# Delta rule in a four-layer kernel: chunks in two halves by turns, small sums in PSUM, query sums on TensorE, waves in half steps

## The chip, the cores and the metric

The kernel runs on one core of a Trainium2 chip. It is written out instruction by instruction: TensorE (PE) multiplies matrices into PSUM, VectorE (DVE) and ScalarE (ACT) work on SBUF and PSUM, GpSimd (POOL) works on SBUF alone, and SyncE (SP) issues most DMAs. The metric is the device time of one execution in microseconds.

## The reference

Four transformer-like layers work on 4096 tokens of 128 features. The change lies in the fourth, which adds two branches to its input: a gated delta rule with 16 heads of 8 dimensions, and a feed-forward network with a sine in it. Cut to what matters:

```python
def step(S, inp):                       # 1024 steps, 4 x 16 independent heads, S is 8 x 8
    q_t, k_t, v_t, b_t = inp
    v_new = (v_t - einsum('bhd,bhdm->bhm', k_t, S)) * b_t[..., None]
    S = S + einsum('bhd,bhm->bhdm', k_t, v_new)
    o_t = einsum('bhd,bhdm->bhm', q_t, S)
    return (S, o_t)
...
imag = w_imag * sin(theta + hidden * 0.1)          # hidden = x @ W1 + b1, 512 wide
q = hidden + (cos(theta) * w_real + sin(theta) * w_imag) * imag * 0.1
out = relu(q) @ W2 + b2
```

Queries and keys are divided by their norms over the 8 dimensions. The outputs of a head are normalised afterwards and multiplied by a last matrix.

## The kernel before

**The delta rule.** The 1024 steps are cut into 32 chunks of 32 steps (`CH` and `N` in `_delta_rule`, L1749). All chunks go through their steps side by side. A state tile has 128 partitions (head and batch, times two halves of the 8 value dimensions) and 1024 columns: 32 chunks of 4 values by 8 key dimensions. It lies in two PSUM banks, chunks 0 to 15 in one and 16 to 31 in the other.

One step of the rule is `differ` (L1853) with `update` (L1868). DVE multiplies the state in PSUM by the keys (`pro`, L1859), and sums the products over the 8 key dimensions (`dd`, L1862). With values it subtracts these (L1865), and it multiplies the difference by the keys (`u`, L1870). PE writes the state anew: `add` (L1847) multiplies a copy of the old state by the identity, and `u` by the negative identity, into the same PSUM tile. Each `add` is two matmuls, one for each bank, and the profile shows two records of each matmul. ACT makes the copy of the state (`copy`, L1874).

Three stretches follow one another on the same tiles:

- The chunk products: 32 iterations (L1898), each with two steps. One (`sm`) turns unit matrices into each chunk's product, the other (`sn`) gives what the chunk makes of a zero state. They alternate, so that PE works on one while DVE works on the other. From the ninth iteration on, `query_norms` (L1889) lets ACT square a block of queries, and DVE reduces the block of the iteration before (L1896, eight times).
- The scan over chunks (L1921): 31 small steps on DVE alone, each two products, a sum and an addition (L1924 to L1932), in SBUF. Ahead of it the rows of `mm` are exchanged between partition halves by DMA, and the inverse norms of the queries are formed (L1917, with the helper at L1783).
- The steps from the scan's states (L1944): 32 steps of the rule for all chunks at once, `pro` in two instructions. In each, GpSimd multiplies the state's copy by the queries (`dprod`, L1965), and DVE sums the products two iterations later (L1941). A one-element GpSimd copy from `u` into `pace` (L1963) stands ahead of the product in GpSimd's queue.

**The waves.** `_waves` (L1970) is the sine network: 32 items of 128 x 512. An item passes through five stages: `enter` (matmul into `qh`, three ACT operations that give argument and number of turns), `fold` (DVE takes off the turns and clamps, L2013 and L2014; ACT forms the sine), `rest` (DVE L2019, ACT Relu), `leave` (matmul into `qo`) and `close` (DVE adds four items' result to `x`, L2030). A wave step runs `close`, `leave`, `rest`, `fold`, `enter`, each on a different item.

**The order.** Layer 3 is recorded under `manual_schedule` (L2105): PE, DVE, ACT and POOL run their instructions in the order in which Python issues them, and the tile layer adds only semaphores. A wait therefore holds everything behind it on its engine. Two accesses of different engines to one PSUM bank are put one after the other. `_delta_rule` is a generator, and the loop at its call decides after which of its yields a wave step follows:

```python
for n, _ in enumerate(_delta_rule(k, s, wl)):
    if n % 2 if n < 32 or n >= 63 else n % 6 == 2:
        next(waves, None)
```

Yields 0 to 31 are those of the chunk products, 32 to 62 those of the scan, and the later ones those of the last 32 steps. The wave steps fall 16 in the first stretch, 6 beside the scan and 14 in the last.

Of the kernel before, what the change touches and what calls it, by code (L numbers as in the profile page):

```python
# [20 lines left out]
P = 128  # L21
# [196 lines left out]
def _bc(ap, axis, n):  # L218

    ap = ap.unsqueeze(axis)  # L220
    shape = list(ap.shape)
    shape[axis] = n
    return ap.to_broadcast(shape)
# [1525 lines left out]
def _delta_rule(k, s, wl):  # L1749
# [7 lines left out]
    CH = 32  # L1757
# [89 lines left out]
    def add(st, w, u, first, last):  # L1847

        c = u.shape[1]
        for n in (slice(0, 16), slice(16, c)):  # L1850
            nc.tensor.matmul(st[:, n], w, u[:, n], start=first, stop=last)  # L1851

    def differ(st, now, i, c, values, parts=1):  # L1853


        pro = room("pro")
        for n in range(parts):
            own = slice(n * c // parts, (n + 1) * c // parts)
            nc.vector.tensor_tensor(pro[:, own], st[:, own], _bc(kp[:, i, own], 2, 4), ALU.mult)  # L1859
        add(st, k.ident, now()[:, :c], True, False)  # L1860
        d = w.tile([P, CH, 4], F32, name="dd")
        nc.vector.tensor_reduce(d[:, :c], pro[:, :c], AX.X, ALU.add)  # L1862
        yield
        if values:
            nc.vector.tensor_tensor(d[:, :c], d[:, :c], vp[:, i, :c], ALU.subtract)  # L1865
        yield update(st, d, i, c)

    def update(st, d, i, c, first=False):  # L1868
        u = room("u")
        nc.vector.tensor_tensor(u[:, :c], _bc(d[:, :c], 3, 8), _bc(kp[:, i, :c], 2, 4), ALU.mult)  # L1870
        add(st, k.neg_ident, u[:, :c], first, True)
        return u

    def copy(name, st, c):  # L1874
        now = room(name)
        nc.scalar.copy(flat(now[:, :c]), flat(st[:, :c]))  # L1876
        return now
# [6 lines left out]
    ends = CH - 1  # L1884
    add(sm, k.ident, _bc(k.unit.rearrange("p (v d) -> p v d", d=8), 1, ends), True, True)
    mm, nn = copy("hist", sm, ends), None
    squares = ip.tile([P, 4, 8, P], F32, name="dvo")

    def query_norms(c):  # L1889
        if 0 <= c < 8:  # L1890
            own = slice(c * P, (c + 1) * P)
            nc.scalar.activation(squares[:, c % 4], qraw[:, :, own], AF.Square)
        if 1 <= c < 9:
            own = slice((c - 1) * P, c * P)
            sq = squares[:, (c - 1) % 4]
            nc.vector.tensor_reduce(rq[:, own], sq.rearrange("p d t -> p t d"), AX.X, ALU.add)  # L1896

    for i in range(N):  # L1898
        for _ in differ(sm, lambda: mm, i, ends, False):
            pass  # L1900
        mm = copy("hist", sm, ends)
        if i:
            for _ in differ(sn, lambda: nn, i, ends, True):
                pass
        else:
            d = w.tile([P, CH, 4], F32, name="dd")
            nc.vector.tensor_scalar(d[:, :ends], vp[:, 0, :ends], -1.0, None, ALU.mult)
            update(sn, d, 0, ends, True)
        nn = copy("dprod", sn, ends)
        query_norms(i - 8)  # L1910
        yield

    both = [room("u") for _ in range(2)]
    for m in range(2):
        for other in range(2):
            nc.sync.dma_start(both[m][HALF[other], :ends], mm[HALF[m], :ends])
    inverse(rq)  # L1917
    nc.vector.tensor_scalar(rq, rq, 8.0**-0.5, None, ALU.mult)
    start = ip.tile([P, L], F32, name="from_unit").rearrange("p (c v d) -> p c v d", v=4, d=8)
    nc.vector.memset(start[:, 0], 0.0)  # L1920
    for c in range(CH - 1):  # L1921
        pro = w.tile([P, 4, 2, 4, 8], F32, name="scan")
        for m in range(2):
            nc.vector.tensor_tensor(  # L1924
                pro[:, :, m],
                _bc(both[m][:, c], 1, 4),
                _bc(start[:, c, :, 4 * m : 4 * m + 4], 3, 8),
                ALU.mult,
            )
        r = w.tile([P, 4, 8], F32, name="scan_r")  # L1930
        nc.vector.tensor_reduce(r, pro.rearrange("p v m j d -> p v d (m j)"), AX.X, ALU.add)  # L1931
        nc.vector.tensor_tensor(start[:, c + 1], r, nn[:, c], ALU.add)  # L1932
        yield
    oc = ip.tile([P, N, CH, 4], F32, name="dvo")
    st = states("sm")
    add(st, k.ident, start, True, True)
    q_at = qraw.rearrange("p d (c i) -> p c d i", i=N)
    hist, prod = None, None

    def output(i):  # L1940
        nc.vector.tensor_reduce(oc[:, i], prod, AX.X, ALU.add)  # L1941


    for i in range(N + 1):  # L1944
        if i < N:
            hist = None

            def now():
                nonlocal hist
                hist = copy("hist", st, CH) if i else start  # L1950
                return hist

            step = differ(st, now, i, CH, True, 2)
            next(step)
            yield
            u = next(step)
        else:
            u, hist = None, copy("hist", st, CH)
        if i >= 2:
            output(i - 2)  # L1960
        if i:
            if u is not None:
                nc.gpsimd.tensor_copy(s.pace, u[:, 0, 0, 0:1])  # L1963
            prod = room("dprod")
            nc.gpsimd.tensor_tensor(prod, hist, _bc(q_at[:, :, :, i - 1], 2, 4), ALU.mult)  # L1965
    output(N - 1)
# [3 lines left out]
def _waves(k, a, s):  # L1970
# [26 lines left out]
    nc.vector.scalar_tensor_tensor(argb, k.vec("l3_b1"), 0.1, theta, ALU.mult, ALU.add)  # L1997
    b1 = k.vec("l3_b1")
# [3 lines left out]
    def enter(z):  # L2002
        z.one = slice(z.f, z.f + 1)
        z.hp = s.q_ps.tile([P, W], F32, name="qh")
        nc.tensor.matmul(z.hp, w1[:, z.f * P : (z.f + 1) * P], k.xn[:, z.c], start=True, stop=True)
        z.arg = xp.tile([P, W], F32, name="qarg")
        nc.scalar.activation(z.arg, z.hp, AF.Identity, bias=argb[:, z.one], scale=0.1)
        z.turns = xp.tile([P, W], F32, name="qtmp", bufs=2)
        nc.scalar.activation(z.turns, z.arg, AF.Identity, bias=rnd[:, 0:1], scale=1.0 / TWO_PI)
        nc.scalar.activation(z.turns, z.turns, AF.Identity, bias=rnd[:, 1:2])  # L2010

    def fold(z):
        nc.vector.scalar_tensor_tensor(z.arg, z.turns, -TWO_PI, z.arg, ALU.mult, ALU.add)  # L2013
        nc.vector.tensor_scalar(z.arg, z.arg, PI_F32, -PI_F32, ALU.min, ALU.max)  # L2014
        nc.scalar.activation(z.arg, z.arg, AF.Sin)
# [18 lines left out]
    stages = (enter, fold, rest, leave, close)  # L2034
    for n in range(len(items) + 4):
        for m in (4, 3, 2, 1, 0):
            if 0 <= n - m < len(items):
                stages[m](items[n - m])
        yield
# [47 lines left out]
def _layer3(k, a, out):  # L2087
    nc, tc = k.nc, k.tc
    with ExitStack() as stack:
# [17 lines left out]
        s.pace = s.ip.tile([P, 1], F32, name="pace")  # L2107
        with ExitStack() as banks:
# [6 lines left out]
            s.st_ps, s.q_ps, s.q_out = bank("st_ps", 1), bank("q_ps", 3), bank("qo_ps", 1)  # L2115
            waves = _waves(k, a, s)
            for n, _ in enumerate(_delta_rule(k, s, wl)):
                if n % 2 if n < 32 or n >= 63 else n % 6 == 2:
                    next(waves, None)
# [80 lines left out]
```

## Time and profile before

| what | us |
|---|---|
| median of three runs | 4837.96 (4836.27 to 4839.41) |
| profiled execution | 4844.06 |
| its span | 4842.3 |
| from the first `pro` to the last `u` of the chunk products | 281.8 |
| from there to the scan | 16.7 |
| scan | 52.0 |
| from the first `pro` to the last `u` of the last steps | 241.3 |
| from there to the output's scaling | 8.9 |

Over the whole span PE is busy 81%, DVE 65%, ACT 53% and POOL 14%, but most of this is in the layers before. In the listings, a timeline's line gives the start (us from the span's start), the duration, the engine, the line of the kernel, the operation, and output and inputs by tile; the brackets at the end give the idle time of the engine before it and what released it. Consecutive instructions of one kind may be merged (x2). Successive DVE instructions overlap a little, so that the time from one start to the next is what counts. In the groups, busy time and mean duration (ns) stand after the bar.

### The profile page before, as it was taken

The page shows a single profiled execution, that of the slowest core. Times are in us where ns is not written, and L with a number is a line of the kernel's source. Part 1 is how long each engine was busy: PE and PEld are TensorE (multiplying, and loading weights), DVE is VectorE, ACT ScalarE, POOL GpSimd, SP SyncE. Part 2 cuts the span into 40 slices and gives each one's busy share as a digit, 9 for nine tenths or more (in the row PEclk, how much of TensorE's full clock was granted, in tenths as well). Part 3 has the DMA queues.
Part 4 walks back from the last instruction along what each step waited for, and adds up shares of the span by engine and source line. Part 5 has one row for each costly group of instructions (what it writes and reads, how often), then busy time and mean ns, then how long its engine had stood idle before and what let it go on. Part 6 is the DMA issues. An engine that isn't in the chain of part 4 may idle for free. (4 is left out here: it accounts for less than half of the span.)

```text
span 4842.3 us, 54404 instructions
## 1 busy us (share of the span) xinstructions
PE 3915.2 (81%) x20918; PEld 1780.8 (37%) x20918; DVE 3134.4 (65%) x4431; ACT 2564.8 (53%) x3611; POOL 660.3 (14%) x647
## 2 busy tenths in 40 slices
PE   4679999998968888888877888888776975889565
PEld 3223333364422222222224555555432453333121
DVE  4868989622345565656558888887572323799876
ACT  1257877831269999999965555545311110344331
POOL 1310000003100000000003223232004023000132
PEclk6689999999967777777779999999888986999788
DMA  2412120021221010100011111111001122400001
GB/s 106 117 40 58 25 63 20 11 77 43 12 81 57 18 57 9 53 18 18 9 58 32 35 36 42 35 37 31 20 3 45 44 73 60 121 0 9 0 0 52
DMA packets 112742, 196.99 MB, mean 41 GB/s; under 512 B 23266, under 2 KB 53474, under 8 KB 110498
## 3 DMA queue, kind: packets, MB, share of 16 engines
q1 hardware_dynamic: 103860, 168.86, 12.4%
q0 software_dynamic: 8192, 16.79, 1.8%
q10 hardware_dynamic: 432, 7.86, 0.4%
q8 instruction: 165, 2.70, 0.2%
q14 instruction: 93, 0.76, 0.1%
HBM read 97.56 MB, written 70.01 MB: 35 GB/s over the span
## 5 line engine op out<-in xcount | busy, mean ns | idle before, releaser
L738 DVE TENSOR_TENSOR p<-p,e 128x1024 f32<-128x1024 f32 x512 | 586.6, 1222 | 322.3 <-ACT e L736 322.3
L721 PE MATMUL big<-q,k 32*128 32x512 f32 x2048 | 561.2, 633 | 180.4 <-ACT p L732 75.4
L531 DVE TENSOR_REDUCE m<-mx 128x2 f32<-128x1024 f32 x512 | 620.9, 1224 | 101.7 <-PE mx L523 94.3
L416 PE MATMUL av<-p,v 128*32 128x256 f32 (+1 forms) x5632 | 667.0, 530 | 0.2
L614 ACT ACTIVATE p<-s 128x512 f32<-128x512 f32 x1024 | 551.6, 598 | 187.0 <-PE s L605 173.0
L721 PEld LDWEIGHTS big<-q,k 32*128 32x128 f32 x2048 | 210.3, 229 | 708.1 <-ACT e L736 353.6
L605 PE MATMUL s<-q,k 64*128 64x512 f32 x1024 | 278.6, 494 | 46.6 <-DMA q<-mrows 31.7
L736 ACT ACTIVATE e<-big,neg_mu 128x1024 f32<-128x1024 f32 x256 | 262.2, 1126 | 11.8 <-PE big L721 11.6
L523 PE MATMUL mx<-k,q 64*128 64x512 f32 x1024 | 239.4, 437 | 32.3 <-DVE m L531 17.9
L732 ACT ACTIVATE p<-big,neg_mu 128x1024 f32<-128x1024 f32 x256 | 261.3, 1198 | 3.5 <-PE big L721 3.3
L736 ACT ACTIVATE e<-big 128x1024 f32<-128x1024 f32 x256 | 242.8, 1042 | 28.0 <-PE big L721 26.9
L732 ACT ACTIVATE p<-big 128x1024 f32<-128x1024 f32 x256 | 239.6, 1076 | 8.4 <-PE big L721 8.2
L1163 POOL TENSOR_TENSOR lqk<-lt 128x512 f32<-128x512 f32 x128 | 162.6, 1270 | 517.9 <-DVE lt L1154 460.8
L1136 PE MATMUL lps<-f_wqkv,lh 128*128 128x512 f32 x384 | 215.3, 649 | 11.1 <-DVE lo L1291 6.8
L1851 PE MATMUL sm<-hist,in_const_sb 128*128 128x512 f32 x252 | 140.6, 686 | 92.7 <-ACT hist L1876 79.1
L416 PEld LDWEIGHTS av<-p,v 128*32 128x32 f32 x5632 | 121.1, 112 | 254.6 <-issue 203.2
L605 PEld LDWEIGHTS s<-q,k 64*128 64x128 f32 x1024 | 108.0, 184 | 284.6 <-issue 162.5
L1017 POOL DMA_INDIRECT cl_row<-res,back x128 | 121.5, 949 | 621.9 <-DMA in_l_su_sb<-in_l_su 476.0
L1254 ACT ACTIVATE lsm<-lsm 128x512 f32<-128x512 f32 x128 | 80.9, 632 | 221.8 <-DVE lsm L1253 220.3
L1876 ACT COPY hist<-sm 128x992 f32<-128x992 f32 (+1 forms) x65 | 65.0, 1000 | 216.4 <-DVE pro L1859 133.6
L936 POOL DMA_INDIRECT buf<-xtok,to x128 | 123.7, 966 | 359.2 <-DVE gkern L1609 169.7
L1129 POOL MEMSET lva<- 128x32 f32 x16 | 2.4, 151 | 1147.9 <-PE av L416 1147.9
(403 smaller groups left out, 6960.5 us busy)
## 6 DMA issues: line engine op xcount, KB each, us to landing
hl<-phi SPq DMA_DIRECT2D x64, 256.0 KB
hl<-plo SPq DMA_DIRECT2D x64, 256.0 KB
lvs<-lva SPq DMA_DIRECT2D x16, 520.0 KB
q<-hl SPq DMA_DIRECT2D x32, 256.0 KB
k<-hl SPq DMA_DIRECT2D x32, 256.0 KB
q<-hl SPq DMA_DIRECT2D x16, 512.0 KB
k<-hl SPq DMA_DIRECT2D x16, 512.0 KB
buf<-zeros ACTq DMA_DIRECT2D x3, 2560.0 KB
```

What stands on the lines that cost most here:

```text
L416: k.nc.tensor.matmul(av[32 * j : 32 * j + 32, cols], v[:, kc, 9 * (4 * g + j) : 9 * (4 * g + j) + 32], pts[j][:, cols], start=kc == 0, sto ...
L523: nc.tensor.matmul(ps[:, i, :], q[rows, gg, qt * P : (qt + 1) * P], key[rows, gg, half * W : (half + 1) * W], start=True, stop=True, tile_ ...
L531: nc.vector.tensor_reduce(m[:, qt, gg, :, half], ps, AX.X, ALU.max)
L605: nc.tensor.matmul(ps, key[rows, half, kc * P : (kc + 1) * P], q[rows, half, qh * W : (qh + 1) * W], start=True, stop=True, tile_position= ...
L614: nc.scalar.activation(p, ps, AF.Exp, scale=8.0**-0.5)
L721: nc.tensor.matmul(ps[:, jj, :], key[rows, kc * P : (kc + 1) * P], q[rows, qh * W : (qh + 1) * W], start=True, stop=True, tile_position=(3 ...
L732: nc.scalar.activation(p, ps, f, bias=bias, scale=scale)
L736: nc.scalar.activation(e, ps, f, bias=bias, scale=scale)
L738: nc.vector.tensor_tensor(p, p, e, ALU.mult)
L1136: nc.tensor.matmul(ps, z.h[:, t * P : (t + 1) * P], wqkv[:, own], start=True, stop=True)
L1163: nc.gpsimd.tensor_tensor(z.qk[t][:, own], r[0], r[1], ALU.add)
L1851: nc.tensor.matmul(st[:, n], w, u[:, n], start=first, stop=last)
```

## The change

- In the last 32 steps, each step is made once for chunks 0 to 15 and once for 16 to 31 (`own`), each half with its own bank: `pro`, copy, identity `add`, `dd`, subtraction, `u`, negative `add`. The output sum and a yield stand behind the first half. The loop has 33 rounds with two yields each. `pace` is gone.
- The small sums `dd` of all stretches, and those of the scan, are written to PSUM, to four slices by turns (`turn`) of one tile in one bank. The scan's states are written straight to the PSUM tile `sm`, from which the last steps go on; the `add` that carried them there is gone.
- The queries' squares are summed by eight matmuls with the identity into such a slice, and ACT copies the result to `rq`. The square root follows in the 19th iteration of the chunk products. Behind them, one DVE operation clamps and scales, and a reciprocal follows.
- In the waves, argument and turns are kept in units of a turn, so that `fold` becomes a plain subtraction on GpSimd. The clamp and the sine are a new stage `sine`. A wave is two half steps with a yield each: `close`, `leave`, `rest`, `sine`, and then `enter`, `fold`. A half step follows every odd yield, and every yield of the scan: 16 half steps in the chunk products, 31 beside the scan, and the last 25 (of 72) in the last steps. `qh` has two PSUM buffers instead of three, `dd` takes the bank.

```diff
-    def add(st, w, u, first, last):
-        c = u.shape[1]
-        for n in (slice(0, 16), slice(16, c)):
-            nc.tensor.matmul(st[:, n], w, u[:, n], start=first, stop=last)
-    def differ(st, now, i, c, values, parts=1):
+    turns = itertools.cycle(range(4))
+    dd = s.d_ps.tile([P, 4, CH, 4], F32, name="dd")
+    turn = lambda: dd[:, next(turns)]
+    def add(st, w, u, own, first, last):
+        for n in (slice(0, 16), slice(16, CH)):
+            n = slice(max(n.start, own.start), min(n.stop, own.stop))
+            if n.start < n.stop:
+                nc.tensor.matmul(st[:, n], w, u[:, n], start=first, stop=last)
+    def differ(st, now, i, own, values):
         pro = room("pro")
-        for n in range(parts):
-            own = slice(n * c // parts, (n + 1) * c // parts)
-            nc.vector.tensor_tensor(pro[:, own], st[:, own], _bc(kp[:, i, own], 2, 4), ALU.mult)
-        add(st, k.ident, now()[:, :c], True, False)
-        d = w.tile([P, CH, 4], F32, name="dd")
-        nc.vector.tensor_reduce(d[:, :c], pro[:, :c], AX.X, ALU.add)
-        yield
+        nc.vector.tensor_tensor(pro[:, own], st[:, own], _bc(kp[:, i, own], 2, 4), ALU.mult)
+        add(st, k.ident, now(), own, True, False)
+        d = turn()
+        nc.vector.tensor_reduce(d[:, own], pro[:, own], AX.X, ALU.add)
         if values:
-            nc.vector.tensor_tensor(d[:, :c], d[:, :c], vp[:, i, :c], ALU.subtract)
-        yield update(st, d, i, c)
+            nc.vector.tensor_tensor(d[:, own], d[:, own], vp[:, i, own], ALU.subtract)
+        update(st, d, i, own)
...
         if 1 <= c < 9:
             own = slice((c - 1) * P, c * P)
-            sq = squares[:, (c - 1) % 4]
-            nc.vector.tensor_reduce(rq[:, own], sq.rearrange("p d t -> p t d"), AX.X, ALU.add)
+            sums = turn().rearrange("p c v -> p (c v)")
+            for d in range(8):
+                nc.tensor.matmul(sums, k.ident, squares[:, (c - 1) % 4, d], start=d == 0, stop=d == 7)
+            nc.scalar.copy(rq[:, own], sums)
...
         query_norms(i - 8)
+        if i == 18:
+            nc.scalar.activation(rq, rq, AF.Sqrt)
         yield
...
-    inverse(rq)
-    nc.vector.tensor_scalar(rq, rq, 8.0**-0.5, None, ALU.mult)
-    start = ip.tile([P, L], F32, name="from_unit").rearrange("p (c v d) -> p c v d", v=4, d=8)
-    nc.vector.memset(start[:, 0], 0.0)
+    nc.vector.tensor_scalar(rq, rq, 1e-6, 8.0**0.5, ALU.max, ALU.mult)
+    nc.vector.reciprocal(rq, rq)
+    st = states("sm")
+    nc.vector.memset(st[:, 0], 0.0)
     for c in range(CH - 1):
...
-                _bc(start[:, c, :, 4 * m : 4 * m + 4], 3, 8),
+                _bc(st[:, c, :, 4 * m : 4 * m + 4], 3, 8),
                 ALU.mult,
             )
-        r = w.tile([P, 4, 8], F32, name="scan_r")
+        r = turn().rearrange("p c v -> p (c v)")[:, :32].rearrange("p (v d) -> p v d", d=8)
         nc.vector.tensor_reduce(r, pro.rearrange("p v m j d -> p v d (m j)"), AX.X, ALU.add)
-        nc.vector.tensor_tensor(start[:, c + 1], r, nn[:, c], ALU.add)
+        nc.vector.tensor_tensor(st[:, c + 1], r, nn[:, c], ALU.add)
         yield
-    st = states("sm")
-    add(st, k.ident, start, True, True)
+    both_halves = slice(0, CH // 2), slice(CH // 2, CH)
...
     for i in range(N + 1):
-        if i < N:
-            hist = None
-            def now():
-                nonlocal hist
-                hist = copy("hist", st, CH) if i else start
-                return hist
-            step = differ(st, now, i, CH, True, 2)
-            next(step)
-            yield
-            u = next(step)
-        else:
-            u, hist = None, copy("hist", st, CH)
-        if i >= 2:
-            output(i - 2)
+        hist = room("hist")
+        for half, own in enumerate(both_halves):
+            if i < N:
+                differ(st, lambda: copy(hist, st, own), i, own, True)
+            else:
+                copy(hist, st, own)
+            if half == 0 and i >= 2:
+                output(i - 2)
+            if half == 0:
+                yield
         if i:
-            if u is not None:
-                nc.gpsimd.tensor_copy(s.pace, u[:, 0, 0, 0:1])
             prod = room("dprod")
             nc.gpsimd.tensor_tensor(prod, hist, _bc(q_at[:, :, :, i - 1], 2, 4), ALU.mult)
+        yield
...
     def fold(z):
-        nc.vector.scalar_tensor_tensor(z.arg, z.turns, -TWO_PI, z.arg, ALU.mult, ALU.add)
-        nc.vector.tensor_scalar(z.arg, z.arg, PI_F32, -PI_F32, ALU.min, ALU.max)
-        nc.scalar.activation(z.arg, z.arg, AF.Sin)
+        nc.gpsimd.tensor_tensor(z.arg, z.arg, z.turns, ALU.subtract)
+    def sine(z):
+        nc.vector.tensor_scalar(z.arg, z.arg, 0.5, -0.5, ALU.min, ALU.max)
+        nc.scalar.activation(z.arg, z.arg, AF.Sin, scale=2.0 * PI_F32)
...
-    stages = (enter, fold, rest, leave, close)
+    at = lambda n: items[n] if 0 <= n < len(items) else None
     for n in range(len(items) + 4):
-        for m in (4, 3, 2, 1, 0):
-            if 0 <= n - m < len(items):
-                stages[m](items[n - m])
-        yield
+        for parts in (((close, 4), (leave, 3), (rest, 2), (sine, 1)), ((enter, 0), (fold, 0))):
+            for fn, m in parts:
+                if at(n - m):
+                    fn(at(n - m))
+            yield
...
-            s.st_ps, s.q_ps, s.q_out = bank("st_ps", 1), bank("q_ps", 3), bank("qo_ps", 1)
+            s.st_ps, s.q_ps, s.q_out = bank("st_ps", 1), bank("q_ps", 2), bank("qo_ps", 1)
+            s.d_ps = bank("d_ps", 1)
             waves = _waves(k, a, s)
             for n, _ in enumerate(_delta_rule(k, s, wl)):
-                if n % 2 if n < 32 or n >= 63 else n % 6 == 2:
+                if 32 <= n < 63 or n % 2:
                     next(waves, None)
```

## The prediction

> **What bounds the kernel now.** The page's chain and its list of costly groups place the code that the diff touches in the last 650 us of a 4842 us span; the layers before it are not touched. I cut that stretch at the landmarks of the timeline and asked for the busy time of each engine in each piece. The columns are: stretch and length, then busy time (instructions) of PE, its weight loads, DVE, ACT and POOL, then the granted PE clock.
>
> ```profile
> 4188.70:4470.50 281.80, 254.67 (x558) 100.93 (x558) 271.81 (x296) 115.96 (x145) 0.00 (x0) 0.99 0.05 10
> 4470.50:4487.20 16.70, 5.61 (x12) 2.12 (x12) 10.33 (x9) 6.49 (x8) 0.00 (x0) 0.80 0.29 61
> 4487.20:4539.20 52.00, 18.99 (x22) 6.71 (x22) 48.81 (x141) 18.29 (x26) 0.00 (x0) 0.63 0.00 1
> 4541.40:4782.70 241.30, 159.74 (x296) 61.47 (x297) 182.18 (x228) 70.61 (x88) 89.88 (x60) 0.90 0.00 0
> 4782.70:4791.60 8.90, 3.61 (x7) 1.25 (x5) 3.53 (x3) 1.01 (x1) 5.84 (x3) 0.88 0.00 0
> ```
>
> They are the chunk products (I call it A), a passage, the scan over chunks (B), the steps from the scan's states (C) and the end. DVE fills A (272 of 282) and B (49 of 52), but only 182 of 241 in C. DVE's timeline in A shows what fills it:
>
> ```profile
> 4288.76 1.19 DVE L1859 TENSOR_TENSOR pro<-sn,dk 128x992 f32<-128x992 f32 x1
> 4289.98 1.19 DVE L1862 TENSOR_REDUCE dd<-pro 128x124 f32<-128x992 f32 x1
> 4291.20 0.29 DVE L1865 TENSOR_TENSOR dd<-dd,dv 128x124 f32<-128x124 f32 x1
> 4291.53 1.19 DVE L1870 TENSOR_TENSOR u<-dd,dk 128x992 f32<-128x992 f32 x1
> 4292.64 1.90 DVE L1896 TENSOR_REDUCE drq<-dvo 128x128 f32<-128x1024 f32 x1
> 4294.45 0.74 DVE L2019 SCALAR_TENSOR_TENSOR qhid<-qarg,q_coef,qh 128x512 f32<-128x512 f32 x1
> 4295.11 0.69 DVE L2013 SCALAR_TENSOR_TENSOR qarg<-qtmp,qarg 128x512 f32<-128x512 f32 x1
> 4295.83 0.43 DVE L2014 TENSOR_SCALAR qarg<-qarg 128x512 f32<-128x512 f32 x1
> ```
>
> No idle is noted in these lines: start to start, 7.42 us of step, 1.82 of query sums (L1896), and 0.66 + 0.72 + 0.34 of a wave. In C there is a gap instead, the 1.02 us of the first line here (a step without a wave, 6.27 us long):
>
> ```profile
> 4772.26 1.29 DVE L1859 TENSOR_TENSOR pro<-sm,dk 128x512 f32<-128x512 f32 x2 [1.02 <-PE sm L1851]
> 4773.59 1.22 DVE L1862 TENSOR_REDUCE dd<-pro 128x128 f32<-128x1024 f32 x1
> 4773.66 1.01 ACT L1876 COPY hist<-sm 128x1024 f32<-128x1024 f32 x1 [5.26 <-DVE pro L1859]
> 4775.17 1.22 DVE L1870 TENSOR_TENSOR u<-dd,dk 128x1024 f32<-128x1024 f32 x1
> 4776.31 1.21 DVE L1941 TENSOR_REDUCE dvo<-dprod 128x128 f32<-128x1024 f32 x1
> ```
>
> C is thus a chain, DVE then PE then DVE, with DVE waiting for the four records of `add`.
>
> **The change, part by part.** Times are start to start from these timelines; a half operation is taken from the 512-wide rows.
>
> *A, moved waves: -17.7.* Up to the last `u`, A held 13 `qhid`, 14 folds with clamps and 2 `x` additions: 13 x 0.66 + 14 x 1.06 + 2 x 0.66 = 24.7. Afterwards only eight waves are begun there, in half steps: 6 x 0.66 + 7 x 0.34 + 0.66 = 7.0. PE has room for the rest (16 records of 0.427 = 6.8 in 7.42).
>
> *A, query sums on PE: -14.6, and a new wait, +24.6.* Eight reductions leave DVE (8 x 1.82). The sums now go to one of four slices of the `dd` tile, all in one bank, and in the built program the next step's `dd` reduction waits for ACT's copy of the sums, eight times. With t = 0 at the end of the step's second `u`: PE's four `add` records end at 2.0; the 16 records of 128 columns follow them from 1.84 at 0.122 each (78.2 us for 640 such records at L991) and land at 4.0; ACT meanwhile copies `nn` (2.04 to 3.03) and squares (1.06, to 4.1), then copies the sums (0.27, as the 128x128 copy of L1000) to 4.4. DVE, which would reduce at 1.14, starts at 4.47. Queued behind that reduction are the subtraction, `u` and so PE. 8 x 3.33, less 2 x 1.0 where a wave's DVE work lies in the gap. Ends: 0 if nothing waits; 8 x 4.9 - 2 = 37 if the records go at the 0.22 of the 128-wide loads at half clock (L295).
>
> *Passage: -9.3.* DVE now sat idle 6.25 us for the square root and its table, then ran 0.69 + 6.55 + 0.69. The root moves into A, where ACT is busy 116 of 282; one clamp-and-scale (0.7) and the reciprocal (6.6) stay: 7.4 for 16.7. The DMAs of `both` (issued at 4469.67, 3.95 us of issue) start where they did, ahead of it.
>
> *B: +21.4.* A scan step is 1.395 (4492.78 to 4494.19). Its waves go from six to 31 half steps; each pair of steps then holds `qhid`, the clamp and a quarter of an `x` addition: 2 x 1.395 - 0.12 + 1.0 + 0.17 = 3.84. But the clamp waits on GpSimd's fold, and DVE's scan queues behind it. With two `qh` buffers instead of three, wave n's matmul waits for `qhid` of n - 2. From that instruction's start: 0.74, PE 2.3 at the half clock seen here (L2005's load at 4547.15 to ACT at 4549.44), ACT 0.70 + 0.75 + 0.72, GpSimd 1.27 (L1163: 1270 ns), hand-offs 0.2: L = 6.7. The clamp stands one period P and 0.66 later, and P = 3.84 + wait, so the wait is (6.7 - 3.84 - 0.66)/2 = 1.1 and P = 4.9; at full clock L = 5.7, P = 4.45. I take 4.8, nearer the half clock because B's mean now is 0.63: 15 x 4.8 + 1.4 = 73.4 for 52.0. Ends: 59 with no wait, 101 if each pair took all of L. The last half step ahead of C costs +0.5.
>
> *C, halves: 241.3 becomes 223.3, -18.0.* A half is `pro` 0.72, `dd` 0.72, subtraction 0.25, `u` 0.61 = 2.30; two and the output (1.14) make 5.74. PE's answer for one half (0.05 + 2 x 0.43 + 0.38 = 1.3; 2.2 at half clock) now lies under the other half's 3.4 us of DVE work, so the 1.02 goes. GpSimd's product (2.86), no longer paced by `u`, starts 1.43 after the second `pro` and ends at 4.3, and is wanted at 4.6. Late next are wave steps: in eight steps (i = 2 to 16) ACT's three activations stand ahead of the second half's copy, and the fold stands ahead of the product in GpSimd's queue. From the end of the first `u`: PE 2.07, ACT to 4.27, fold 4.35 to 5.62, product to 8.5; the next step's output, due at 5.6, waits 3.0, and some 0.15 is lost in the step after. Sum: 32 x 4.60 + 30 x 1.14 + waves on DVE 11.7 + 8 x 3.15 = 218.3, and 5 for half clock (1.75 in about three of ten, by the 0.90). Ends: -25 without these waits, +9 with the half clock in all.
>
> *End: -2.6.* After the last `u`: PE 1.3, half a copy 0.6, product 2.9, output 1.25, hand-offs 0.2 = 6.3 for 8.9.
>
> *Sums in PSUM: 0.* 473 DVE instructions (157 in A, 124 in B, 192 in C) gain a PSUM operand. `tensor_tensor` of 512 takes 688 ns from PSUM (L1147) and 692 from SBUF (L1253); a 1024 reduction 1224 (L531) and 1220 (L1862). Against it, `scalar_tensor_tensor` takes 746 with PSUM (L1393) and 689 without (L1609): +57 ns, 27 us over 473. No row writes PSUM from DVE, so the ends are 57 ns either way; I take the rows of the same operations, zero.
> [...]
>
> *GpSimd beside DVE: 0.* L1204, with two SBUF inputs while GpSimd works, takes 1069 ns on the mean instead of 692. In the changed loops each such product, difference and sum has one input in PSUM, as `pro` has now: at 4772.26 it ran beside GpSimd's product of 4770.39 (2.86 us) at its usual length. If that cover failed, 64 half `u` in C at +0.38 would cost 24. The convolutions, down from three to two `qh` buffers, are continuous on PE and keep a spare one: 0, at worst 0.1 at each of 32 tiles.
>
> **Sum.** -17.7 - 14.6 + 24.6 - 9.3 + 21.9 - 18.0 - 2.6 = -15.7. The profiled execution took 4844.1 (span 4842.3 and 1.8 around it), so 4828.4; it stands 6.1 above the median 4838.0, on which I forecast 4822. About 0.2% (9.7 us) is what a measurement of this kernel tells from no change.
>
> **Rivals.** *The waits bind less:* PE warms up in B and the next output is late by less: B at 59 (-14) and half of C's 25 gone: some -42, 4796. B's clock of 0.63 speaks against. *The waits bind more:* query records at 0.22 (+12) and half clock at every wave in C (+9): +5, 4843, no change; the clock of 0.99 in A speaks against the first. *PSUM operands cost 57 ns each* in the DVE-bound stretches, which are nearly all of it after the change: +27 - 15.7 = +11, 4849, slower. It undoes the gain at 33 ns and makes it a loss that can be measured at 54 ns; the `tensor_tensor` rows speak against it, the missing row of a PSUM write leaves it open.
>
> **How the numbers follow.** Forecast 0.45 (own range 4808 to 4830), binding less 0.15, binding more 0.22, PSUM cost 0.18. The low end lies by the second case (4796), the high end at the last (4850). Faster: 0.43 of the forecast, all of the second, 0.02 of the rest = 0.60. Slower: most of the PSUM case and 0.04 of "more": 0.20. Same: 0.20.
>
> **What would show it.** Right: A near 274, with eight gaps of about 3.3 us ahead of a `dd` reduction, released by ACT's copy of `drq`; passage near 7.4; B near 73 with about 1 us of DVE idle ahead of each clamp, released by GpSimd; C's steps near 5.7 us without waves and an output late by 3 us after each fold. Wrong: a reduction of 992 into `dd` away from 1.19 us, or a scan step away from 1.40 us between waves (PSUM cost); no gap at the query sums; a bare step in C above 6.3 us.

## The result: 0.8% slower

The changed kernel took 4873.66 us (median; 4871.71 to 4887.05), the kernel before 4837.49 (four runs of each). The ratio is 1.0081, with a 95% interval of 1.0064 to 1.0098. A second pair of the same two kernels on another chip gave 1.0101 (1.0084 to 1.0117). The forecast was 4822 in a range of 4796 to 4850, so the time lies outside it, and on the wrong side of the kernel before.

The profiled execution of the changed kernel took 4875.05 us with a span of 4873.2. Here are the busy times by stage, in the layout and order of the table before: stretch and length, busy time of PE, its weight loads, DVE, ACT and POOL, granted PE clock, DMA.

```profile
4176.80:4448.30 271.50, 249.27 (x656) 110.78 (x656) 240.78 (x260) 96.95 (x119) 8.88 (x7) 0.99 0.05 10
4448.30:4455.60 7.30, 3.65 (x8) 1.44 (x8) 7.22 (x4) 3.02 (x4) 1.26 (x1) 1.00 0.66 139
4455.60:4534.70 79.10, 44.76 (x60) 14.68 (x60) 58.64 (x160) 50.85 (x76) 19.02 (x15) 0.72 0.00 0
4534.70:4814.10 279.40, 180.76 (x296) 55.17 (x294) 192.76 (x309) 67.81 (x112) 97.61 (x40) 0.87 0.00 0
4814.10:4820.70 6.60, 1.22 (x3) 0.30 (x2) 2.48 (x3) 1.07 (x2) 4.72 (x2) 0.82 0.00 0
```

A and the passage came out short, as forecast, and the scan (B) long, as forecast. The fourth line is the surprise. C takes 279.4 us instead of the 223.3 forecast, and DVE is busy in only 192.8 of them. What DVE waits for, over all these stretches (total us, times, longest; two waits below 0.5 us are left out):

```profile
DVE pro L1865 <- PE sm L1858: 79.9, 58, 5.0
DVE dd L1868 <- ACT drq L1903: 22.6, 8, 3.1
DVE pro L1865 <- ACT hist L1879: 17.8, 3, 15.9
DVE qarg L2017 <- POOL qarg L2014: 17.7, 15, 3.0
DVE dvo L1948 <- POOL dprod L1964: 4.1, 2, 2.2
```

The second and fourth lines are the new waits that the prediction named, in their number and about in their size (8 for 24.6 us, and 15 of about 1.1 us). In the third, 15.9 us are one wait that ends with the first `pro` of A. The first line was not in it: `pro` waits for PE 58 times in 64. The timeline of a bare step in C, with PE's weight loads left out:

```profile
4759.93 0.69 DVE L1865 TENSOR_TENSOR pro<-sm,dk 128x512 f32<-128x512 f32 x1 [1.77 <-PE sm L1858]
...
4761.65 0.69 DVE L1875 TENSOR_TENSOR u<-dd,dk 128x512 f32<-128x512 f32 x1
...
4762.40 1.12 PE L1858 MATMUL sm<-u,neg_ident 128*128 128x512 f32 x2
4763.63 0.69 DVE L1865 TENSOR_TENSOR pro<-sm,dk 128x512 f32<-128x512 f32 x1 [1.29 <-PE sm L1858]
...
4765.35 0.69 DVE L1875 TENSOR_TENSOR u<-dd,dk 128x512 f32<-128x512 f32 x1
4765.96 1.21 DVE L1948 TENSOR_REDUCE dvo<-dprod 128x128 f32<-128x1024 f32 x1
...
4766.09 1.12 PE L1858 MATMUL sm<-u,neg_ident 128*128 128x512 f32 x2
4767.33 0.69 DVE L1865 TENSOR_TENSOR pro<-sm,dk 128x512 f32<-128x512 f32 x1 [0.16 <-PE sm L1858]
```

The second `pro` (4763.63) belongs to the other half, whose bank PE had written before 4759.93. Yet it starts right after PE's last `add` for the half that began at 4759.93 (4762.40 + 1.12 = 4763.52). The halves run one after the other: twice the chain `pro`, `dd`, subtraction, `u`, PE, 3.70 us each. A step takes 7.40 us, where whole steps took 6.27.

Between the first pair of profiles, the stages differ like this (us; A and C end with their last `u`):

| stretch | before | after | difference | forecast |
|---|---|---|---|---|
| layers ahead (to `pair`, the layer's first DVE work) | 4050.2 | 4027.6 | -22.6 | 0 |
| layer norm and convolutions, to the first `pro` | 138.5 | 149.3 | +10.8 | 0 |
| A, chunk products | 281.8 | 271.4 | -10.4 | -7.7 |
| passage | 16.7 | 7.3 | -9.4 | -9.3 |
| B, scan, to the first `pro` of C | 54.2 | 79.2 | +25.0 | +21.9 |
| C, to the last `u` | 241.3 | 279.4 | +38.1 | -18.0 |
| from there to the last output sum | 7.7 | 5.3 | -2.4 | -2.6 |
| after it | 51.9 | 53.8 | +1.9 | 0 |

### The profile page after: what moved, and what is told of

It reads as the page before. It is cut to its first block, busy times and chain, and to the rows that moved or that the text cites. A ratio compares the mean times of both kernels' runs of the same rounds, so it can differ in the third digit from the quotient of the medians.

```text
span 4873.2 us, 54832 instructions
## 1 busy us (share of the span) xinstructions
PE 3947.7 (81%) x21042; PEld 1791.5 (37%) x21042; DVE 3117.5 (64%) x4487; ACT 2567.9 (53%) x3653; POOL 697.9 (14%) x648
## 5 line engine op out<-in xcount | busy, mean ns | idle before, releaser
L524 PE MATMUL mx<-k,q 64*128 64x512 f32 x1024 | 239.2, 437 | 31.3 <-DVE m L532 17.8
L1858 PE MATMUL sm<-hist,in_const_sb 128*128 128x512 f32 (+1 forms) x256 | 145.8, 674 | 105.5 <-ACT hist L1879 98.6
L1879 ACT COPY hist<-sm 128x512 f32<-128x512 f32 (+1 forms) x99 | 70.8, 716 | 242.0 <-DVE pro L1865 146.1
```

The costliest lines, as they stand in the source:

```text
L524: nc.tensor.matmul(ps[:, i, :], q[rows, gg, qt * P : (qt + 1) * P], key[rows, gg, half * W : (half + 1) * W], start=True, stop=True, tile_ ...
```

## The experiments

Each kernel was timed against the kernel before on its own chip. That kernel took 4832 us on the chip of the first four and 4773 to 4779 on the others; the ratios and the stages inside a profile are what compare. Absolute times in the expectations are meant for the first of these chips.

### Two state tiles

The halves get a PSUM tile each (`sn` is free when the scan begins), and the scan reads `at(c)` and writes `at(c + 1)`.

```diff
-    st = states("sm")
+    parts = states("sm"), states("sn")
+    at = lambda c: parts[c // 16][:, c]
...
         for half, own in enumerate(both_halves):
+            st = parts[half]
```

> The changed kernel with the states of the last 32 steps in two PSUM tiles, chunks 0 to 15 in one and 16 to 31 in the other; nothing else differs. The changed kernel took 4873.7, with 278 us from the first `pro` to the last `u` of these steps and 7.40 us for a bare step. Theory 1 (the tile layer orders accesses to one tile, not to one bank, so that each half's `pro` waits for the other half's last `add`): bare step 5.8 us, no DVE idle ahead of `pro` in bare steps, stretch 225 to 240, time 4820 to 4836. Theory 2 (PE's answer to a half is late by itself, whatever the tile): bare step stays at 7.4, time 4870 to 4877. Theory 3 (the wave steps set the stretch): bare steps fall to 5.8, steps with waves stay, stretch 250 to 262, time 4845 to 4858.

Measured: 4826.68 us, ratio 0.9984 (0.9969 to 1.0000); C takes 226.6 us. The timeline of a bare step in C (`sm` is the first half, `sn` the second):

```profile
4728.02 0.68 DVE L1865 TENSOR_TENSOR pro<-sm,dk 128x512 f32<-128x512 f32 x1
...
4728.15 1.13 PE L1858 MATMUL sn<-u,neg_ident 128*128 128x512 f32 x2
4728.73 0.69 DVE L1868 TENSOR_REDUCE dd<-pro 128x64 f32<-128x512 f32 x1
...
4730.34 1.21 DVE L1949 TENSOR_REDUCE dvo<-dprod 128x128 f32<-128x1024 f32 x1
...
4730.47 1.13 PE L1858 MATMUL sm<-u,neg_ident 128*128 128x512 f32 x2
4731.46 0.68 DVE L1865 TENSOR_TENSOR pro<-sn,dk 128x512 f32<-128x512 f32 x1
...
4733.78 0.68 DVE L1865 TENSOR_TENSOR pro<-sm,dk 128x512 f32<-128x512 f32 x1
```

No idle is noted on DVE; PE writes `sn` while DVE works on `sm`, and a step takes 5.76 us instead of 7.40. Theory 1 holds: the order is kept for the PSUM tile as a whole, not for each of its banks, and a separate tile gives 52.8 us of C back. What is said of one PSUM bank in the description of the kernel before thus holds, in these kernels, for a whole tile of two banks. The waits that are left in C are those that the prediction had named, the output behind the fold, eight times:

```profile
DVE dvo L1949 <- POOL dprod L1966: 27.3, 8, 4.5
DVE pro L1865 <- PE sn L1858: 2.3, 1, 2.3
DVE qarg L2019 <- POOL qarg L2016: 1.7, 2, 1.5
DVE pro L1865 <- PE sm L1858: 0.5, 1, 0.5
```

### Whole steps again

In C alone, `pro` in two pieces, one copy, one `add` of two matmuls, the rest of the change kept.

```diff
-        for half, own in enumerate(both_halves):
-            if i < N:
-                differ(st, lambda: copy(hist, st, own), i, own, True)
+        every = slice(0, CH)
+        if i < N:
+            differ(st, lambda: copy(hist, st, every), i, every, True, both_halves)
```

> The changed kernel with the last 32 steps made whole again, `pro` in two pieces and one `add` of two matmuls, as before the change; sums in PSUM, query sums on TensorE and the waves' places stay changed. Theory 1 (making the steps in halves on one tile is what cost the time): bare step 6.3 us, stretch 240 to 250 instead of 278, time 4835 to 4846. Rival (the small sums in PSUM, the product no longer paced, or the folds on GpSimd lengthen this stretch): stretch above 265, time above 4860.

Measured: 4853.25 us, ratio 1.0034 (1.0012 to 1.0056); C 245.3. The stretch is inside its range, the time 7 us above. Against the first profile of the kernel before, the layer is 21 us longer: convolutions +9.8, A -8.6, passage -9.4, B +25.3, C +4.0. So splitting the steps on one tile cost 34 us of C, and splitting them on two tiles gains 19 over whole steps. Some 8 us of C lie in the waves here: their ten clamps take 1205 ns on the mean instead of 420, because nine of them (0.61 to 2.78 us) start beside GpSimd's product and end just after it (more on this below). As an estimate, splitting would have cost 42 on one tile and gained 11 on two without that.

### Sums in SBUF

`dd` and the scan's sums go back to SBUF; the query sums keep the PSUM bank alone.

```diff
-        d = turn()
+        d = w.tile([P, CH, 4], F32, name="dd")
...
-        r = turn().rearrange("p c v -> p (c v)")[:, :32].rearrange("p (v d) -> p v d", d=8)
+        r = w.tile([P, 4, 8], F32, name="scan_r")
```

> The changed kernel with the sums `dd` and those of the scan in SBUF, as before the change; the query sums have the PSUM bank to themselves. Theory 1 (a sum in PSUM costs DVE nothing, but sharing the bank makes the next `dd` reduction wait for ACT's copy of the query sums, 22.6 us in eight waits): the eight waits go, chunk products 271 to 249, the other stretches stay within 3 us, time 4848 to 4854. Rival 1 (operands in PSUM cost DVE about 57 ns each): 473 instructions get shorter as well, time 4824 to 4846, and a reduction to `dd` of 992 gets shorter than the 1.19 us it takes in PSUM. Rival 2 (DVE instructions with two SBUF inputs get slow beside GpSimd's): the 64 `u` of the last steps go from 0.69 to 1.07 us, time 4866 to 4878.

Measured: 4967.97 us, ratio 1.0277 (1.0247 to 1.0308). All the theories missed this, by 90 us and more. A took 260.3 instead of 271.4: the eight waits for `drq` are gone (22.6), but 8.6 of that come back as `pro` waiting for the copy of `hist` (26.4 us instead of 17.8), because PE, with four `add` of 1.67 us and query sums of 1.8 in a step of 8.44, is now the limit (248 busy of 260). B stayed at 79.1. C went from 279.4 to 385.5. Its timeline:

```profile
4841.94 1.13 PE L1858 MATMUL sm<-hist,in_const_sb 128*128 128x512 f32 x2 [1.82 <-ACT hist L1879]
4841.97 2.85 POOL L1964 TENSOR_TENSOR dprod<-hist,raw 128x1024 f32<-128x1024 f32 x1 [10.09 <-ACT hist L1879]
4842.03 2.87 DVE L1870 TENSOR_TENSOR dd<-dd,dv 128x64 f32<-128x64 f32 x1
4844.93 0.69 DVE L1875 TENSOR_TENSOR u<-dd,dk 128x512 f32<-128x512 f32 x1
...
4849.31 0.22 DVE L1870 TENSOR_TENSOR dd<-dd,dv 128x64 f32<-128x64 f32 x1
```

The subtraction, 0.22 us alone (4849.31), has two SBUF inputs here. Started just after GpSimd's product, it ends when the product ends (4842.03 + 2.87 = 4844.90; 4841.97 + 2.85 = 4844.82). With `dd` in PSUM it has one SBUF input and takes 0.23 beside the same product (4768.78 in the changed kernel, product from 4768.72). So in this step the DVE instruction with two SBUF inputs, begun second, stood until GpSimd's, which reads SBUF as well, was done. The groups of C, in this kernel:

```profile
L1875 DVE TENSOR_TENSOR u<-dd,dk 128x512 f32<-128x512 f32 x64 | 59.7, 932 | 2.2
L1870 DVE TENSOR_TENSOR dd<-dd,dv 128x64 f32<-128x64 f32 x64 | 59.4, 928 | 2.2
L1865 DVE TENSOR_TENSOR pro<-sm,dk 128x512 f32<-128x512 f32 x64 | 44.2, 691 | 126.8 <-PE sm L1858 126.8
```

and in the changed kernel:

```profile
L1865 DVE TENSOR_TENSOR pro<-sm,dk 128x512 f32<-128x512 f32 x64 | 44.2, 691 | 80.0 <-PE sm L1858 79.9
L1875 DVE TENSOR_TENSOR u<-dd,dk 128x512 f32<-128x512 f32 x64 | 44.2, 691 | 2.2
...
L1870 DVE TENSOR_TENSOR dd<-dd,dv 128x64 f32<-128x64 f32 x64 | 14.9, 232 | 2.2
```

The 106 us are 44.5 of subtraction, 15.5 of `u`, and 46.9 of longer waiting for PE, whose granted clock fell from 0.87 to 0.69 in this stretch. How much of the waiting the clock makes is not shown: PE also stood for `u` (in the timeline above from 4843.07 to the end of `u` at 4845.62), which it never did in C of the changed kernel.

The same runs price a sum in PSUM. A reduction of 992 takes 1195 ns into PSUM (the changed kernel) and 1186 into SBUF (this one), one of 512 takes 695 and 686, `u` 1192 in both. That is 9 ns for some of the instructions, not 57 for all.

### Two tiles and sums in SBUF

The edits of the first and the third experiment together.

> Both edits together: the states of the last steps in two PSUM tiles, and the sums `dd` and those of the scan in SBUF. If the two causes are separate, their gains add: about 4797 to 4813, faster than both kernels. If DVE, once it is full in the last steps, is slowed by GpSimd's products beside instructions with two SBUF inputs (1.07 us instead of 0.69 for 64 `u`), 4815 to 4835.

Measured: 4889.22 us, ratio 1.0112 (1.0085 to 1.0139); C 296.2. Neither range held it, for the same reason: the expectation counted 0.38 us at each `u` and nothing at the subtraction. On the mean, the collision costs 0.36 at each `u` (1054 ns for 691) and 0.57 at each subtraction (805 ns for 233). Against the two tiles alone, C grew by 69.6: subtractions 36.6, `u` 23.1, output waits 9.5.

### The kernel before without `pace`

The kernel before has both inputs of its subtraction in SBUF too, yet the subtraction takes 0.29 us there. If the reading above is right, something must have kept it from the collision.

```diff
-            if u is not None:
-                nc.gpsimd.tensor_copy(s.pace, u[:, 0, 0, 0:1])
```

> The kernel before, without the one-element GpSimd copy from `u` into `pace`. Theory 1 (a DVE instruction with two SBUF inputs stands still until a running GpSimd product ends, which cost 2.6 us a step with sums in SBUF; `pace` had kept the product behind `u`): the subtraction in the last steps goes from 0.29 to about 2.8 us, the stretch from 241 to 310 to 330, time 4905 to 4925. Theory 2 (the long subtractions come only with halves): the subtraction stays below 0.5 us, the stretch 235 to 245, time 4826 to 4838.

Measured: 4855.91 us, ratio 1.0170 (1.0153 to 1.0187); C 320.5 instead of the 241.3 to 243.0 of two profiles with `pace`. The time is 83 us above that of the kernel before, where the expectation meant 73 to 93. Its subtractions in C took 1968 ns on the mean (289 before; about 2.8 us were expected), its folds there, with two SBUF inputs as well, 2386 (686 before). A step of it:

```profile
4713.26 2.85 POOL L1963 TENSOR_TENSOR dprod<-hist,raw 128x1024 f32<-128x1024 f32 x1 [6.04 <-ACT hist L1876]
4713.35 2.91 DVE L1865 TENSOR_TENSOR dd<-dd,dv 128x128 f32<-128x128 f32 x1
...
4716.30 1.22 DVE L1870 TENSOR_TENSOR u<-dd,dk 128x1024 f32<-128x1024 f32 x1
```

So the 0.18 us copy into `pace` held the product back until DVE's instructions with two SBUF inputs were through: in the kernel before, `u` ends at 4770.11, the copy starts at 4770.25 and the product at 4770.39. The change removes `pace`, and the move of `dd` to PSUM takes over its work (0.23 us beside the product). These two edits belong together. Sums in SBUF with `pace` kept were not tried.

### The betas

In the convolution stretch of the changed kernel, these lines stand around the beta rows:

```profile
4085.08 0.68 DVE L1746 COPY dprod<-qh 16x512 f32<-16x512 f32 x1 [0.18 <-PE qh L1745]
...
4086.14 0.56 SPq L1774 DMA_DIRECT2D raw<-rows_k  x1
4090.98 1.27 DVE L1746 COPY dprod<-qh 16x512 f32<-16x512 f32 x2 [5.21 <-DMA rows_b<-dprod]
...
4091.71 18.89 PE L1724 MATMUL qh<-xn,tap_w 128*128 128x512 f32 x40 [4.86 <-DVE dprod L1746]
```

The last two beta sums lie in `qh` and wait for a free `dprod`, whose transfer isn't done. With two `qh` buffers they hold both, and the convolution behind them on PE stands. With three, it had a buffer left. The edit gives each batch its own part of the tile `vraw` (`ys`):

```diff
-        y = s.room("dprod")[:16]
+        y = ys[:16, b]
```

> Two state tiles as in the first experiment (4826.7 there), and the four rows of betas go to four quarters of the tile `vraw`, which is not used yet, instead of two turns of `dprod`. Theory (with two `qh` buffers, both are held by beta sums whose copies wait for the transfer of `dprod` to end, and PE stands for 4.9 and 5.8 us): these two waits go, and the stretch from the layer's start to the first `pro` is 138 instead of 148 us, time 4814 to 4819. Rival (the convolutions themselves want a third `qh` buffer): the stretch stays within 2 us of 148, time 4824 to 4829.

Measured (two state tiles as well): 4762.31 us, ratio 0.9976 (0.9967 to 0.9986). The stretch took 130.7 us, where two kernels without the edit took 137.1 and 137.4 (the next experiment, and the last pair). PE's wait for `dprod` is gone, and three later kernels with the edit took 129.2 to 130.7, so the rival, by which the stretch stays as it was, is out. But 6.4 us came of it, not 10. The theory counted one wait twice: the 4.9 us of PE and the 5.8 of its weight load are idle time ahead of the same matmul, both up to 4091.71. The cause of the other 4 us by which the convolutions are longer than in the kernel before stays open; a third `qh` buffer may be worth them elsewhere. Against two tiles alone the ratio fell by 0.0008, less than the intervals can tell; the gain is shown by the stretches alone.

### Waves later in a step

```diff
-        for parts in (((close, 4), (leave, 3), (rest, 2), (sine, 1)), ((enter, 0), (fold, 0))):
+        for parts in (((close, 4), (leave, 3), (rest, 2), (sine, 1), (hidden, 0)), ((enter, 0), (fold, 0))):
...
-                if 32 <= n < 63 or n % 2:
+                if 32 <= n < 63 or n % 2 == (n < 32):
```

`hidden` is the first matmul of `enter`, moved ahead by half a wave step.

> Two state tiles as in the first experiment, and in the last steps the wave's half step follows the second half of a step instead of the first; the wave's first matmul is issued one half step earlier than its three activations. Theory (the activations ahead of the second copy and the fold ahead of GpSimd's product make the output late, 27.3 us in eight waits): the waits of the output for GpSimd fall below 6 us, the stretch of the last steps goes from 227 to 204 to 210 (33 steps of 5.76 and about 14 us of wave work on DVE), time 4804 to 4812. Rival (wherever they stand, the activations hold a copy up, and the wait only moves to `pro` or to the next step): stretch 220 to 230, time 4820 to 4830.

Measured (two state tiles as well): 4747.72 us, ratio 0.9947 (0.9930 to 0.9963). Against two tiles alone that is 0.0037 less, some 18 us. C 202.7, a little below its range; no output waits for GpSimd any more. All of DVE's waits from 15 us ahead of C to its end:

```profile
DVE qarg L2021 <- POOL qarg L2018: 4.9, 4, 2.6
```

The theory holds: late outputs behind the fold were what waves cost in C with two tiles, and placing the half step behind the product removes that. The first matmul was moved as well; which of the two moves did it was not taken apart.

The new place has a price of its own. The ten clamps in C take 13.1 us instead of 4.2, because nine of them now start while GpSimd's product runs:

```profile
4509.35 2.86 POOL L1966 TENSOR_TENSOR dprod<-hist,raw 128x1024 f32<-128x1024 f32 x1 [1.66 <-ACT hist L1879]
...
4510.95 1.55 DVE L2021 TENSOR_SCALAR qarg<-qarg 128x512 f32<-128x512 f32 x1
```

The product ends at 4512.21 and the clamp at 4512.50. So a clamp stands beside the product too (1.55 us, where one without the product takes 0.42), although it has only one input.

### All four, and then fewer waves beside the scan

The two state tiles, the betas and the later waves, and `dd` in SBUF in the chunk products alone, where GpSimd has little to do:

```diff
-        d = turn()
+        d = w.tile([P, CH, 4], F32, name="dd") if own is ends else turn()
```

> Two state tiles, the betas in `vraw`, the waves of the last steps later, and in the chunk products alone the sums `dd` in SBUF, so that the query sums have the PSUM bank to themselves there. If the four causes are separate, against the first experiment: convolutions -10, chunk products -11 (260 instead of 272), last steps -17 to -23; time 4781 to 4791, 0.8 to 1.1% faster than before. If a gain is only passed on to the next wait, above 4800.

Measured: 4729.90 us, ratio 0.9907 (0.9891 to 0.9924), inside the 0.8 to 1.1% expected. A 259.9, B 79.5, C 203.0. The convolutions gave 6.4 us, not 10 (130.7 for the 137.1 of the kernel with the later waves, on the same chip). The granted clock in C is now 0.99.

The next kernel has no wave beside the scan, and the one after it ten half steps there:

```diff
-                if 32 <= n < 63 or n % 2 == (n < 32):
+                if n % 2 if n < 32 else n >= 63:
```

> The kernel with all four edits (0.9907 of before), but no wave beside the scan: its 31 half steps follow in the last steps, one after every half, 56 in all. Theory (beside the scan a half step costs 1.17 us, because each clamp waits for the chain over PE, the activations and GpSimd; in the last steps, where two halves overlap, it costs only its 0.58 us of DVE work): scan 79.5 to 44, last steps 203 to 223, both 283 to 267, ratio to before 0.987 to 0.988. Rival (with a whole wave in every step, the activations or GpSimd become the limit there): last steps above 235, ratio 0.990 or more.

Measured: 4706.61 us, ratio 0.9847 (0.9831 to 0.9864); B 43.6, C 214.5.

```diff
-                if 32 <= n < 63 or n % 2 == (n < 32):
+                if n % 2 if n < 32 else n >= 63 or n % 3 == 0:
```

> The same with ten half steps beside the scan, one after every third of its steps, so that a clamp stands 4.2 us and more behind its wave's entry and not 1.4; 46 half steps in the last steps. Theory: scan 50 to 55, last steps 215 to 220, both together 266 to 273, ratio 0.987 to 0.988, as without any wave there. Rival (one entry's chain of 5.7 to 6.7 us is longer than two such gaps leave): clamps wait 2 us and more for GpSimd, scan above 58.

Measured: ratio 0.9846 (0.9830 to 0.9863), the same; 4705.78 us where the kernel before took 4779.18. The scan and C of this kernel:

```profile
4389.50:4438.10 48.60, 17.01 (x18) 5.19 (x18) 45.51 (x136) 16.86 (x25) 6.33 (x5) 0.61 0.00 0
4438.10:4647.40 209.30, 170.02 (x336) 55.75 (x336) 200.28 (x334) 98.00 (x163) 110.36 (x50) 0.99 0.00 0
```

Both do better than their theory. Beside the scan, 31 half steps cost 79.5 - 43.6 = 35.9 us, or 1.16 each, as expected. In C, the same 31 lengthen the stretch by only 214.5 - 203.0 = 11.5 us, 0.37 each for the 0.58 expected. The clamps of C show why, in the kernel with all four edits and in the one without scan waves:

```profile
L2021 DVE TENSOR_SCALAR qarg<-qarg 128x512 f32<-128x512 f32 x10 | 13.1, 1311 | 0.5 <-POOL qarg L2018 0.5
L2021 DVE TENSOR_SCALAR qarg<-qarg 128x512 f32<-128x512 f32 x25 | 10.5, 420 | 2.0 <-POOL qarg L2018 2.0
```

With a half step behind every half, no clamp starts beside GpSimd's product any more, and the 8.9 us that they lost are back. Without this, as an estimate, the 31 half steps would have cost 20.4 us, 0.66 each. No theory had counted it: this part of the gain was luck. Both versions are 1.5% faster than the kernel before, and DVE is busy for 200 of the 209 us of C.

### The pair again

> The changed kernel unaltered, once more, on one chip with the next one, to see how the layers ahead of the change stand in both. Up to the layer's start, the first profiles had 4027.6 us for the changed kernel and 4050.2 for the one before, though the order of instructions there is the same. Theory (that difference is scatter between executions): here the two starts lie within 8 us, the changed layer is longer by 48 to 56, and the ratio is 1.009 to 1.012. Rival (the layers ahead do run faster in the changed kernel): its start is 15 us or more earlier again, ratio 1.007 to 1.009.

> The kernel before, unaltered, for its profile on the same chip. Same theories as for the changed kernel: the start of the layer within 8 us of that of the changed kernel, or 15 us and more later.

Measured: 4822.77 us against 4774.71, ratio 1.0101 (1.0084 to 1.0117). The layer starts at 3995.6 in the changed kernel and at 3988.8 in the one before, 6.8 us apart with the other sign, so the 22.6 us between the first profiles is scatter of the layers ahead. The layer is longer by 44.2, a little under the range: convolutions +10.3, A -9.4, passage -9.4, B +25.6, C +27.3 (270.3 for 243.0), the rest -0.3. C was 9 us shorter here than in the first profile: `pro` waited 71.3 us for PE instead of 79.9. The reason is open.

## Why the prediction was wrong

**The step that failed is in C:** "PE's answer for one half (...) now lies under the other half's 3.4 us of DVE work, so the 1.02 goes". It took two banks for two things that can be in work at once. They are one tile, and the second half's `pro` stood behind the first half's `add`. The bare step was forecast at 5.74 us, measured at 7.40, and 5.76 with two tiles. So the arithmetic of DVE was right, and its condition was not met. It cost 52.8 us of C; with two tiles C took 226.6 for the 223.3 forecast, and the ratio of 0.9984 is near the 0.997 of the forecast. (The layer itself is then as long as before, 792.0 us for 792.1. Of the forecast gain of 15.7 us, 9.4 are lost in the convolutions.) The trace before held the sign:

```profile
4770.28 1.88 PE L1851 MATMUL sm<-u,neg_ident 128*128 128x512 f32 x4
```

The first piece of `pro` at 4772.26 touches only the first bank, yet it started after the last of these four records of `add` (4772.16), with the idle time of 1.02 us noted. Had it waited for its own bank, it would have started two records earlier. The prediction read this line as a wait for four records and did not ask why the first piece waited for all of them.

**Convolutions, "0, at worst 0.1 at each of 32 tiles":** +10.8 and +10.3. The third `qh` buffer was not spare at the betas, where a DMA decides when a buffer comes free. The experiment on the betas shows that wait and removes it, which is 6.4 us; the cause of the other 4 stays open.

**Chunk products, -7.7:** -10.4 and -9.4. The new wait for ACT's copy was forecast at 24.6 and came as 22.6, in eight pieces.

**Passage, -9.3:** -9.4.

**Scan, +21.9:** +25.0 and +25.6. The period was forecast as 4.8 us; it came as 5.2, with 15 waits of 1.2 us for GpSimd, which are those foreseen. (A scan step of 1.395 us is misread: its two starts are 1.41 apart. That is below 0.5 us in all.)

**Waves in C, 8 x 3.15:** in the changed kernel the term shows differently (the activations delay the copy, and `pro` waits up to 5 us). With two tiles, it is there as forecast, 27.3 us in eight waits.

**Sums in PSUM, 0:** right by the rows: 9 ns on the reductions, which write PSUM (1195 ns for 1186, 695 for 686), and none on `u`, which reads its sum there (1192 in both). The 57 ns of the rival do not show on these.

**GpSimd beside DVE, 0:** right, and for the reason given, one input in PSUM (`u` took 691 ns, and 932 on the mean with its sum in SBUF). The price of losing that cover was wrong: "would cost 24", and it was 106 us, 60 of them on DVE and 47 in longer waits for PE. The prediction took a mean (1069 ns in L1204) for the price of one collision; in the runs the instruction stood until GpSimd's had ended, and the subtraction, which was not counted, stood longest (2.87 us beside a product of 2.85). Nor did it see that `pace`, which the change drops, was the same cover in the kernel before.

The rivals were all about sizes (waits, clock, PSUM). None asked whether the change does what it says in C. That was the case to name. The list of signs did have it, "a bare step in C above 6.3 us", but with no cause beside it.

## What to carry over

The halves of a step overlapped here only when each had its own tile (a step of 5.76 us, 7.40 on one tile); look in the trace for a piece that waits for more than it reads, and give each half its own tile. A subtraction with two SBUF inputs lost nearly a whole GpSimd product here (2.87 us for 0.22, beside a product of 2.85), and a clamp with one input 1.1 us (1.55 for 0.42); look at the durations as well as at the waits, since such a loss is noted as busy time. Before removing something that seems idle, like a one-element copy in a queue, ask what it keeps apart. Where a buffer is taken from a pool, find the place in the whole layer where all of them are held at once, above all by something that waits for a transfer.

## What was not expected of the hardware

- A subtraction of 0.22 us took 2.87 beside a GpSimd product of 2.85 when both its inputs were in SBUF, and 0.23 when one was in PSUM. A clamp of 0.42 us, with its one input and its output in SBUF, took up to 1.6 beside the same product with the waves later.
- The granted PE clock in C was 0.69 with the sums in SBUF, 0.87 in the changed kernel, 0.91 with two tiles and 0.99 with all four edits. PE was busy for 60, 65, 73 and 77% of C in these. The 296 matmul records of C kept PE busy for 231.3 us in the first of them, and for 180.8 in the second. But the busy share did not settle the clock: the kernel before had 0.90 at 66%, two tiles with sums in SBUF 0.80 at 66%.
- The layers ahead, with the same instructions in the same order, ended at 4027.8 to 4043.1 us in four kernels on one chip, and at 3988.8 to 3995.6 in the eight profiles of the later runs.
